# A four-layer graph network on one core: the first feed-forward layer reads unstrided, and the order of work is drawn up anew

## The chip, the core and the metric

The kernel runs on one core of a Trainium2 chip. TensorE (PE) multiplies matrices, VectorE (DVE) and ScalarE (ACT) do elementwise work, GpSimd (POOL) does small sums and issues software DMAs, SyncE (SP) issues most DMAs. SBUF holds tiles of 128 partitions; PSUM has eight banks, into which TensorE writes. The metric is the device time of one execution in microseconds; less is better. Before the change the median of three runs is 2790.44 us (2789.14 to 2792.24).

## What is computed

64 graphs of 256 nodes with 256 features go through four layers; each is followed by a residual and a normalization. The reference, cut to the part that the change touches and the names of the rest:

```python
# layer 0: transformer block, 8 heads, masked by adj, adj transposed or the diagonal
attn_out = ctx @ Wo.T + bo
x = _layernorm(x + attn_out, ln1_g, ln1_b)
ff = jax.nn.relu(x @ W1.T + b1) @ W2.T + b2      # W1: 1024 x 256, W2: 256 x 1024
x = _layernorm(x + ff, ln2_g, ln2_b)
...
x = _layernorm(x + _L0_gnn_ref(x, adj, ...))     # attention and feed-forward
x = _layernorm(x + _L1_gnn_ref(x, adj, ...))     # graph attention, leaky ReLU, softmax
x = _layernorm(x + _L2_gnn_ref(x, adj, ...))     # graph attention, then ELU
x = _layernorm(x + _L3_gnn_ref(x, ..., adj, adj))  # two relation convolutions with ELU
```

All products are fp32. One fp32 matmul appears in the profile as two records; the gathers of layer 3 use a format in which one record is one matmul.

## The kernel before

One graph is some 190 operations: loads, transposes, products, activations. The program does not run them graph after graph. `graph(g)` only notes each operation in a list, with its engine, an assumed cost, the tiles it reads and writes, and for a DMA an assumed delay. Then `Plan.schedule` plays the list through with these assumed costs and gives each engine its order; the instructions are issued in that order and each engine runs its own queue strictly in it. Among the operations that are ready an engine takes the one with the smallest due date. A due date is `DUE[kind] + LATER[graph]`, two tables of numbers written into the file; for TensorE a switch of the array's mode is added, weighted by `WORTH`. Tiles live in rings (`RINGS`) of fixed depth, and the eight PSUM banks are one ring, so an operation may also wait until a buffer is free. Several graphs are in work at once. `LOADED`, `SENT`, `BACK`, `SENT_ROW` and `BACK_ROW` are the assumed delays of DMAs.

TensorE works in modes: `full` for ordinary products (`product`, line 786), `row` for the scores of attention, in which four heads use 32 rows of the array each (line 882), `col` for the values block (lines 903 and 908), `one` for the gathers of layer 3 (line 1066), `bits` for the four transposes that turn the mask (line 824).

Before a product the activations have to lie transposed. For the graphs 0 to 58 this goes through DRAM (`bounced`): DVE transposes 32 x 32 blocks into `turned`, one DMA writes `rows`, a second reads them back as `T`. In `T` the 256 nodes of a graph stand interleaved: column 2m+i is node m of half i. The last `QUICK` = 5 graphs use transposes on TensorE instead, in natural order. `bounced` returns the tile and a function that gives a product its slice:

```python
return xT, lambda kb, i: xT()[:, kb].rearrange("p (m i) -> p i m", i=NB) if i is None else xT()[:, kb, i::NB]
```

With `i` given, the slice is the stationary operand (128 columns, every second one). With `i` None it is the moving operand of the first feed-forward layer, all 256 columns, first the even and then the odd ones, so that the hidden activations `hid` come out in natural order. ACT applies ReLU and writes `hid` (line 943). The second layer takes 128 columns of `hid` at a time as its stationary operand, through `product_plus`, which also serves the product with `Wo`:

```python
y = product_plus(lambda c: hid()[:, c, :], [hid, c_w2], lambda c: w2[:, c, :], NF, x1)
```

Setup loads weights: `wqkv` by twelve DMAs on ACT's queue, and what has to match the block order (`spread`) by four DMAs each on SP's queue.

Of the kernel before, what the change touches and what calls it, by code (L numbers as in the profile page):

```python
# [18 lines left out]
P = 128  # L19
# [6 lines left out]
QUICK = 5  # L26

LOADED = 3.2
SENT, BACK = 1.4, 2.2
SENT_ROW, BACK_ROW = 1.7, 3.2  # L30
# [8 lines left out]
WORTH, HOLD, WAIT = 158.14, 0.22, 23878.4  # L39
DUE = [  # L40
    -228.56, -76, -83.88, -152.17, -246.95, 144.67, -73.58, -50.13, -117.26, -62.43, -95.69, -135.64, -139, -295.21, -282.91, -186.21, -208.41, -104.04, -41.69, 132.39,
    -61.27, -165.13, -39.15, -180, -151.62, -359.77, -136.97, -344.63, -320.09, -212.19, -142.72, -99.05, 49.68, -80.11, -92.33, -82.22, -228.49, -162.34, -196.2, -244.91,
    -216.45, -69.88, -156.28, -117.75, -82.85, -52.68, -193.67, -239.33, -167.89, -289.39, -43.68, -114.12, -6.04, -10.42, -77.71, -92.13, -53.68, -111.24, -22.19, 168.32,
    144.59, 51.01, 8.81, 41.24, 84.37, 175.47, -24.19, 84.36, -61.57, 131.34, 85.1, -80.71, -149.2, -75.32, 8.06, 27.39, 8.04, -267.57, -62.37, -17.58,
    -253.26, 102.77, 33.92, 18.35, -42.69, -46.09, -48.28, -230.96, -240.74, -321.05, -358.53, -500.29, -514.2, -396.36, -557.51, -771.93, -457.43, -478.74, -295.12, -293.77,
    -405.7, -476.74, -352.2, -274.57, -467.78, -231.13, -189.12, -188.57, -269.51, 216.71, -414.44, 85, 252.52, -54.65, 70.81, -26.5, -215.89, 59.94, 28.39, -485.41,
    -154.54, 102.66, 140.08, -147.96, -262.57, -356.35, -119.53, -148.1, -119.88, -155.26, -161.9, 91.8, -6.93, 12.94, 85.56, 162.78, 25.66, 214.61, 205.89, -197.51,
    -182.79, -197.06, -200.26, -103.63, -115.59, -259.31, -338.52, -106.34, -259.71, -80.69, -497.88, 3.42, -248.76, -327.25, -97.33, 8.68, -180.16, -368.65, -281.95, -105.3,
    -275.74, -247.06, 65.77, -233.44, -85.19, -421.05, -566.16, -486.26, -486.32, -451.69, -442.06, -437.05, -494.12, -508.08, -524.83, -535.88, -518.97, -502.94, -406.01, -476.79,
    -603.45, -343.11, -627.7, -347.53, -174.47, -215.44, -307.54, -408, -112.1, 303.26, 157.74, -39.8, 33.34, 19.96, -300.13, -276.05, -318.71, -327.57, -173.95, -392.12,  # L50
    -156.12, 76.61, -274.79, -361.2, -404.53, -442.47, -519.09, -319.99, -321.18, -291.94, -277.27, -97.06, -315.75, -207.94, -305.04, -125.76, -110.74, -169.12, 68.43, -298.22,
    116.97, 182.76, 26.52, -52.2, -168.42, -233.58, 74.87, 51.38, 57.3, -105.14, -38.09, -30.98, 220.31, 2.89, -163.07, -66.56, -178.1, -275.21, -285.22, -154.13,
    -215.98, -40.34, -24.02, -336.24, 87.43, 124.72, 139.7, -183.1, 20.61, 134.12, -103.74, -217.56, 72.34, 27.18, -125.06, -29.64, -87.06, 56.18, -184.37, -327.66,
    -254.51, -77.41, -216.61, 145.97, -178.56, 65.18, 121.01, 65.95, -164.16, 71.23, 298.67, 101.42, 119.26, 246.24, -19.2, 157.71, -60.74, -49.1, 141.16, 151.7,
    6.29, -203.23, -214.07, 282.47, 36.1, 97.36, 73.41, -159.5, 105.08, 245.27, 55.33, -78.57, -96.45, -99.32, -111.3, -40.22, -71.72, 20.46, -93.44, -51.8,
    -82.46, -123.38, -63.03, -174.7, -109.33, -99.49, 7.74, 7.8, -100.27, -107.37, 43.65, 17.73, -91.19, -69.85, 137.33, -70.25, -342.89, -70.97, -208.14, -97.55,
    81.62, -137.39, -254.76, -114.68, -104.47, 10.23, -50.26, -110.2, -73.87, -176.91, -55.18, -138.53, -312.94, 43.31, -61.82, -0.72, -61.78, -74.02, -38.63, -29.27,
    -70.14, -28.91, 41.42, -98.59, -63.24, -125.41, -81.33, -172.67, -267.92, -56.4, -90.76, -104.21, -60.25, -75.66, -341.93, -194.02, -95.39, -42.07, -515.83, -135.12,
    -112.03, -64.06, -106.33, 66.32, 27.41, 24.19, 10.28, -179.06, -86.33, -145.89, -86.5, -68.17, -53.55, -89.7, -37.91, -81.15, -35.28, -26.15, -21.73, -82.24,
    -22.52, 98.51, 16.99, -111.93, 0.44, -329.15, -38.71, -35.42, -23.68, 13.05, -99.5, 44.6, -30.29, 23.99, -167.93, -74.84, 17.01, -27.46, 18.86, -60.34,  # L60
    -114.38, -19.34, -16.53, -27.1, -139.34, -170.9, -168.16, -179.31, -94.74, 188.45, -118.11, -19.49, -66.48, -278.07, -211.79, -4.89, 27.98, -71.67, -104.5, 53.68,
    -44.94, -47.55, -0.25, -35.15, -37.03, 35.19, -57.46, 56.74, -104.02, 95.93, -31.72, -130.63, 56.29, -25.11, -41.73, -33.88, 32.01, 54.42, -106.5, 2.29,
    22.41, -85.35, -124.85, 266.99, -151.39, 28.71, -4.56, -69.98, -154.76, -14.62, -93.54, -203.26, -68.22, -64.68, -222.87, -184.46, 22.24, 35.38, -99.64, -117.5,
    9.44, -97.68, -133.82, -144.02, -66.91, -74.28, -268.84, -284.99, -315.31, -82.83, -92.11, -374.61, -350.77, -338.3, -353.53, -241.11, -152.28, -288.49, -134.99, -213.19,
    -254.85, -13.82, 44.42, -100.57, 96.07, 74.78, 30.02, -55.36, 4.56, -111.81, 16.41, -82.19, -24.85, -85.15, -253.62, -68.59, -23.2, -78.67, -106.02, -70.78,
    -139.17, -118.08, -139.23, -106.7, -220.82, 221.79, -174.78, -173.9, -72.04, -68.83, -153.77, 23.12, 35.07, -159.76, -108.02, -215.02, -42.35, -8.63, 122.93, -75.54,
    -137.89, -45.2, 169, -249.18, -107.96, -108.64, -147.3, -191.12, -193.79, -404.95, -144.89, -230.67, -150.37, -341.69, -237.62, -171.13, -128.84, -32.83, -142.37, -174.5,
    24.25, -2.12, -133.1, -67.37, -46.83, 209.67, -75.45, -161.34, 26.56, 15.42, -226.2, -123.98, -84.4, 53.98, -71.36, -93.39, -52.63, 74.55, 20.98, -37.9,
    -33.61, 304.99, 128.28, -35.36, -8.15, -64.1, 70.08, -36.03, -179.68, 65.32, -162.07, 96.39, -98.5, 99.91, -41.91, -8.13, 93.48, 223.91, -125.72, 10.85,
    -6.25, 127.98, -24.34, -126.77, -38.56, -164.97, -105.72, -226.65, 92.67, -210.8, -211.04, -335.06, -144.72, -469.23, -582.94, -517.45, -247.22, -199.88, -352.97, -129.8,  # L70
    -215.39, -302.48, -253.94, -240.91, -172.2, -35.13, -454.21, -275.89, -41.12, 56.56, 0.62, -109.22, -246.09, 42.23, -124.72, 148.9, -51.41, -108.52, -53.6, 133.5,
    -64.45, -325.5, -94.04, -208.16, -52.22, -100.71, 62.82, -48.49, -82.22, -153.66, 106.74, -139.96, -236.91, 39.55, -74.32, -220.41, -111.57, -250.98, -118.14, -140.76,
    -27.16, 105.12, -174.95, 197.59, 133.52, -56.45, 101.7, 52.32, -86.67, -87.41, 90.45, 44.99, 214.52, 52.63, 95.67, 35.23, -0.08, 151.96, 240.56, 64.62,
    -66.41, 70.67, 2.68, 64.12, -67.27, -6.81, 71.85, -75.35, 200.91, 156.95, -17.7, -141.62, 34.42, -6.02, -194.13, 70.67, 127.66, -117.54, -96.88, -108.28,
    -9.58, -218.12, -6.58, -71.34, -95.78, 16.09, -65.95, -549.11, -29.95, 39.22, 72.42, -117.95, -205.75, -307.48, -94.32, -165.63, 103.33, 66.01, -68.27, -73.44,
    -43.77, -158.66, -227.92, -59.71, -138.35, -139.55, -251.65, -490.14, -183.81, -111.55, -85.37, 130.24, -64.12, -46.91, -38.3, 127.07, -58.84, 230.43, 157.99, 301.55,
    63.64, -280.98, 9.33, -222.5, -149.85, -74.3, -65.46, -104.18, -139.2, -72.03, 1.32, 133.39, 37.1, 145.41, 81.35, -29.58, -85.73, 10.69, -89.57, -155.68,
    29.93, -158.69, -136.5, -266.31, -251.57, -293.75, -343.53, -190.33, -56.18, -67.01, -183.21, -434.13, -665.78, -309.53, -266.4, -392.43, -414.51, -479.73, -314.38, -260.66,
    -245.16, -214.44, -183.13, -308.57, -166.82, -268.27, -81.36, -116.17, -113.56, -410.09, -22.4, -28.51, -237.86, -155.5, -168.47, -61.24, -166.35, 7.17, 219.14, -83.62,
    -50.64, -44.88, -138.06, 137.5, 300.41, 144.25, 219.56, -24.29, 17.09, 28.44, 157.58, 16.65, -96.34, 84.39, 88.66, 212.4, -210.93, 44.08, 150.63, -143.62,  # L80
    47.03, -142.86, 3.57, 187.87, -24.54, -25.24, -206.26, -188.72, -46.69, -169.46, -42.43, -0.74, -106.68, 6.23, 98.16, -27.97, -232.56, -82.77, -72.44, -234.93,
# [33 lines left out]
class Plan:  # L115
# [13 lines left out]
    LOOK = 40  # L129
# [68 lines left out]
    def schedule(self):  # L198
        n = self.kinds()
# [1181 lines left out]
```

## Time and profile before

| | |
|---|---|
| median of three runs | 2790.44 us |
| the profiled execution | 2788.03 us, its span 2786.3 us |
| granted TensorE clock | 0.996 |
| first layer, matmul records (`T,w`) | 2048, mean 390 ns |
| second layer, matmul records (`w,hid`) | 2048, mean 379 ns |
| weight loads of layers 1 and 2 (`gw,T`) | 1024, mean 195 ns |
| scores (`bank<-qk`) | 2048 records, 139.4 us busy |
| DMA | mean 119 GB/s |

The profile is one execution. A group's row names the line, engine, operation, output and inputs, then busy time and the mean duration of one. Matmuls overlap: a record's duration is longer than the distance to the next one, so the pace is read from the starts in the timeline. The span in 40 slices shows TensorE at nine tenths or more in all but the first and the last slice.

### The profile page before, as it was taken

The numbers are of one execution on the slowest core, as the hardware profiler recorded it, in microseconds if no ns is written. First come the engines' busy times: TensorE is split into PE (matmuls) and PEld (weight loads), VectorE is DVE, ScalarE is ACT, GpSimd is POOL, SyncE is SP. The second block draws the span as 40 slices with busy tenths as digits, with TensorE's granted clock in tenths as the row PEclk, the third lists the DMA queues.
The fourth block names the chain that finished last, engine by engine and source line by source line (L and its number), as shares of the span: only waits on it lengthen the run. The fifth ranks groups of instructions, "written<-read, shape, count | busy, mean of one in ns | idle before, by whom it ended". The sixth has DMA issues, their size and how long they took to land.

```text
span 2786.3 us, 48831 instructions
## 1 busy us (share of the span) xinstructions
PE 2749.3 (99%) x15790; PEld 2092.4 (75%) x15790; DVE 2498.9 (90%) x6527; ACT 1588.5 (57%) x3827; POOL 819.9 (29%) x1753
## 2 busy tenths in 40 slices
PE   7999999999999999999999999999999999999997
PEld 5877777777777777777777777777777777777774
DVE  6898899999999998999999999989999999999777
ACT  4455555655655555556556555555565565566567
POOL 3223232332332322323323323223233232232232
PEclk9999999999999999999999999999999999999999
DMA  7454554545545545545445455455454454553121
GB/s 191 110 124 122 129 125 114 139 108 125 136 113 132 129 115 134 124 114 139 114 120 139 116 126 133 113 134 122 114 139 115 119 135 104 132 122 85 43 55 43
DMA packets 612637, 330.45 MB, mean 119 GB/s; under 512 B 394488, under 2 KB 603896, under 8 KB 612376
## 3 DMA queue, kind: packets, MB, share of 16 engines
q1 hardware_dynamic: 566856, 275.46, 36.1%
q0 software_dynamic: 44560, 51.01, 12.2%
q8 instruction: 128, 2.10, 0.3%
q14 instruction: 133, 1.09, 0.1%
q10 hardware_dynamic: 960, 0.79, 0.1%
HBM read 183.12 MB, written 94.23 MB: 100 GB/s over the span
## 4 chain that ended last, share of the span: by engine, by line
PE 90%; DVE 4%; DMA 3%; ACT 2%; issue 1%; POOL 0%; ACTq 0%; SPq 0%; POOLq 0%; DVEq 0%
PE bank L786 75%; PE bank L882 4%; PE bank L908 4%; PE bank L1066 4%; PE bank L903 2%; DMA rows<-turned 1%; DMA T<-rows 1%; PE bank L824 1%; DVE p L890 0%; DMA row<-cols 0%; DMA pf<-row 0%; DVE turned L755 0%; DVE e L992 0%; DVE e L995 0%; ACT X L807 0%
## 5 line engine op out<-in xcount | busy, mean ns | idle before, releaser
L786 PE MATMUL bank<-T,w 128*128 128x256 f32 x2048 | 500.7, 390 | 0.0
L800 POOL TENSOR_SCALAR rstd<-mv 128x2 f32<-128x2 f32 x384 | 98.1, 256 | 1284.8 <-DVE mv L797 1144.8
L786 PE MATMUL bank<-cw,T 128*128 128x512 f32 x1024 | 462.7, 593 | 1.0 <-DMA T<-rows 0.4
L786 PE MATMUL bank<-w,hid 128*128 128x256 f32 x2048 | 461.6, 379 | 1.3 <-ACT hid L943 1.3
L807 ACT ACTIVATE X<-X,rstd 128x256 f32<-128x256 f32 x640 | 348.9, 597 | 196.4 <-POOL rstd L803 187.1
L786 PEld LDWEIGHTS bank<-T,w 128*128 128x128 f32 x2048 | 379.5, 188 | 91.7 <-issue 13.9
L786 PEld LDWEIGHTS bank<-w,hid 128*128 128x128 f32 x2048 | 388.3, 190 | 58.1 <-issue 2.7
L890 DVE TENSOR_TENSOR p<-p,am 128x512 f32<-128x512 f32 x512 | 332.1, 681 | 11.0 <-ACT p L888 9.0
L786 PEld LDWEIGHTS bank<-cw,T 128*128 128x128 f32 x1024 | 198.2, 195 | 188.0 <-issue 177.0
L888 ACT ACTIVATE p<-bank 128x512 f32<-128x512 f32 x512 | 300.3, 607 | 35.3 <-PE bank L882 35.3
L801 POOL TENSOR_TENSOR rstd<-rstd,neghalf 128x2 f32<-128x2 f32 x384 | 294.8, 768 | 32.2
L786 PE MATMUL bank<-h,e 128*128 128x259 f32 x1024 | 260.1, 383 | 3.7 <-ACT e L997 3.6
L786 PE MATMUL bank<-xT,wqkv 128*128 128x256 f32 x1024 | 260.5, 390 | 3.0 <-DMA cw<-in_w_root_dram 3.0
L1053 ACT CAST hi<-bank 128x256 fp32r<-128x256 f32 x256 | 95.1, 372 | 275.8 <-PE bank L786 275.8
L786 PE MATMUL bank<-gw,T 128*128 128x258 f32 x1024 | 246.3, 381 | 0.7 <-ACT T L736 0.7
L943 ACT ACTIVATE hid<-bank,col_b 128x256 f32<-128x256 f32 x512 | 216.5, 473 | 45.8 <-PE bank L786 42.3
L795 DVE BATCH_NORM_STATS2 st<-X 128x6 f32<-128x256 f32 x640 | 236.7, 411 | 3.0
L786 PEld LDWEIGHTS bank<-h,e 128*128 128x128 f32 x1024 | 189.3, 190 | 56.6 <-issue 24.9
L786 PEld LDWEIGHTS bank<-xT,wqkv 128*128 128x128 f32 x1024 | 188.7, 191 | 57.3 <-issue 28.4
L914 DVE RECIPROCAL inv<-bank 128x256 f32<-128x256 f32 x128 | 218.6, 1727 | 8.0 <-PE bank L908 7.9
L786 PEld LDWEIGHTS bank<-gw,T 128*128 128x128 f32 x1024 | 196.5, 195 | 27.8 <-issue 3.8
L1080 ACT ACTIVATE e<-o 128x512 f32<-128x512 f32 x128 | 80.6, 630 | 217.8 <-DVE o L1076 215.9
(129 smaller groups left out, 4758.3 us busy)
## 6 DMA issues: line engine op xcount, KB each, us to landing
rows<-turned SPq DMA_DIRECT2D x295, 256.0 KB
T<-rows SPq DMA_DIRECT2D x295, 256.0 KB
adj<-in_adj_dram SPq DMA_DIRECT2D x128, 256.0 KB
blocks<-in_x_dram SPq DMA_DIRECT2D x256, 64.0 KB
x<-in_x_dram SPq DMA_DIRECT2D x64, 256.0 KB
xr<-in_x_dram SPq DMA_DIRECT2D x64, 256.0 KB
xr<-row_ln_b POOLq DMA_DIRECT2D x64, 256.0 KB, 4.4
x<-row_bo POOLq DMA_DIRECT2D x64, 256.0 KB, 4.8
```

The costliest lines, as they stand in the source:

```text
L786: nc.tensor.matmul(dst, lhsT=lhs(c), rhs=rhs(c), start=(c == 0), stop=(c == n - 1))
L795: nc.vector.bn_stats(stat()[:, i, :], y()[:, i, :])
L800: nc.gpsimd.tensor_scalar(rstd()[:, 0, :], mv()[:, :, 1], 1.0, EPS, op0=ALU.mult, op1=ALU.add)
L801: nc.gpsimd.tensor_tensor(rstd()[:, 0, :], rstd()[:, 0, :], neghalf[:, 0:NB], op=ALU.pow)
L807: nc.scalar.activation(y()[:, i, :], y()[:, i, :], AF.Identity, bias=rstd()[:, 1, i : i + 1], scale=rstd()[:, 0, i : i + 1])
L882: nc.tensor.matmul(s[r]()[:, hg, :], lhsT=qk()[f, KB + hg, kt * P : (kt + 1) * P], rhs=qk()[f, hg, :], start=True, stop=True)
L888: act(0.58, lambda pr=pr, k=k, sr=s[r]: nc.scalar.activation(pr(), sr(), AF.Exp, accum_out=seen_sum[:, k : k + 1]), [s[r]], [pr])
L890: dve(0.60, lambda pr=pr, kt=kt: nc.vector.tensor_tensor(pr(), pr(), am()[:, kt, None, :].to_broadcast([P, KB, N]), op=ALU.mult), [pr, am] ...
L908: nc.tensor.matmul(pc[32 * r : 32 * r + 32, 0, :], lhsT=v()[:, kt, HD * h : HD * (h + 1)], rhs=p[kt, r]()[:, hg, :], start=(kt == 0), stop ...
L914: dve(1.67, lambda hg=hg, pc=pc: nc.vector.reciprocal(inv()[:, hg, :], pc()[:, 1, :]), [pc], [(inv, hg)])
L943: act(0.36, lambda f=f, k=k, ph=ph: nc.scalar.activation(hid()[:, f + k, :], ph()[:, k, :], AF.Relu, bias=b1[:, f + k : f + k + 1]), [ph, ...
L1066: nc.tensor.matmul(pa()[:, 0:n], lhsT=rel()[:, i, j * P : (j + 1) * P], rhs=part()[:, i, 0:n], start=(c == 0), stop=(c == len(terms) - 1))
```

## The change

Four parts. No product, activation or vector operation is added or taken away.

1. `bounced` hands out the whole row of `T` as it lies for the first layer, so `hid` keeps the interleaved order. The second layer takes every second column of `hid` as its stationary slice. The last five graphs keep their natural order.
2. `spread` and the loads of `wqkv` are two DMAs over all 128 partitions each, where there were four over 32.
3. The rules of the order: the tables `DUE` and `LATER` and the weights are new, a window limits how far an engine may run ahead of its oldest waiting operation, the two groups of scores of a graph are held together, and the assumed delays of DMAs are longer.
4. A few assumed costs are corrected.

```diff
-LOADED = 3.2
-SENT, BACK = 1.4, 2.2
-SENT_ROW, BACK_ROW = 1.7, 3.2
+LOADED = 3.8
+SENT, BACK = 2.5, 3.0
+SENT_ROW, BACK_ROW = 2.7, 3.7
...
-WORTH, HOLD, WAIT = 158.14, 0.22, 23878.4
+WORTH, HOLD, WAIT, LOCK = 20.0, 0.0, 1000000.0, -0.5
+WINDOW, FIRST, TAIL = 4.0, 6, 58
...
-                for o in ops[: self.LOOK]:
+                while point[e] < len(queue[e]) and queue[e][point[e]].start is not None:
+                    point[e] += 1
+                limit = float("inf")
+                if point[e] < len(queue[e]) and FIRST < queue[e][point[e]].graph < TAIL:
+                    limit = queue[e][point[e]].order[0] + WINDOW
+                if e == "PE" and held:
+                    if now < until:
+                        later.append(until)
+                    else:
+                        held = None
+                for o in ops:
+                    if o.order[0] > limit and o.graph > FIRST:
+                        continue
+                    if e == "PE" and held and o is not held:
+                        continue
...
+                if e == "PE":
+                    if o is held:
+                        held = None
+                    elif o.pair and o.pair.start is None:
+                        held, until = o.pair, now + o.cost + 0.5 + LOCK
...
-                view = (t[name] if rel is None else t[name][rel]).rearrange("(k b c) n -> b c k n", b=4, c=32)
-                for b in range(4):
-                    plan.op("SP", 0.6, lambda b=b: nc.sync.dma_start(to[b::4], view[b]), 0, [], [(w, (name, b))],
-                            size=view.shape[3] / 1024 * 0.9, lag=2.2)
+                view = (t[name] if rel is None else t[name][rel]).rearrange("(k b c) n -> k c b n", b=4, c=32)
+                for k in range(KB):
+                    plan.op("SP", 0.55, lambda k=k: nc.sync.dma_start(to[:, k, :], view[k]), 0, [], [(w, (name, k))],
+                            size=view.shape[3] / 512 * 0.9, lag=2.4)
...
-                return xT, lambda kb, i: xT()[:, kb].rearrange("p (m i) -> p i m", i=NB) if i is None else xT()[:, kb, i::NB]
+                return xT, lambda kb, i: xT()[:, kb, :] if i is None else xT()[:, kb, i::NB]
...
+                groups[0].pair, groups[1].pair = groups[1], groups[0]
...
-                    pe("full", 0.4275 * n + 0.01, lambda i=i: product(po()[:, i, :], lambda c: lhs(c)[:, i * P : (i + 1) * P], rhs, n),
+                    pe("full", 0.4275 * n + 0.01, lambda i=i: product(po()[:, i, :], lambda c: lhs(c, i), rhs, n),
...
-                y = product_plus(lambda c: hid()[:, c, :], [hid, c_w2], lambda c: w2[:, c, :], NF, x1)
+                hid_at = (lambda c, i: hid()[:, c, i::NB]) if g < B - QUICK else (lambda c, i: hid()[:, c, i * P : (i + 1) * P])
+                y = product_plus(hid_at, [hid, c_w2], lambda c: w2[:, c, :], NF, x1)
```

The tables `DUE` (one number for each kind of operation) and `LATER` (64 numbers, one for each graph) are replaced whole and not printed.

## The prediction

> **What bounds the kernel.** I read the page from the top: busy shares, the chain that ended last, the costliest groups, then TensorE's own waits, and last the timeline of TensorE in a window in the middle.
>
> ```profile
> PE 2749.3 (99%) x15790; PEld 2092.4 (75%) x15790; DVE 2498.9 (90%) x6527; ACT 1588.5 (57%) x3827; POOL 819.9 (29%) x1753
> PE 90%; DVE 4%; DMA 3%; ACT 2%; issue 1%; POOL 0%; ACTq 0%; SPq 0%; POOLq 0%; DVEq 0%
> ```
>
> TensorE (PE) holds 90% of the chain that ended last. Its busy share alone would not say so, since matmul ends are modelled; its waits do:
>
> ```profile
> PE bank L679 <- DMA blocks<-in_x_dram: 6.4, 1, 6.4
> PE bank L824 <- DVE ident_b L427: 5.6, 1, 5.6
> PE bank L786 <- ACT e L997: 3.6, 11, 0.7
> PE bank L786 <- DMA cw<-in_w_root_dram: 3.0, 1, 3.0
> ```
>
> The whole list adds up to 24.8 us of 2786.3, and of these four lines all but the third lie in the first 30 us. Between its waits TensorE is never free, so the time is the sum of what its instructions take, and a change is worth what it takes out of that sum or out of those waits. The granted clock is 0.996.
>
> ```profile
> L786 PE MATMUL bank<-T,w 128*128 128x256 f32 x2048 | 500.7, 390 | 0.0
> L786 PE MATMUL bank<-w,hid 128*128 128x256 f32 x2048 | 461.6, 379 | 1.3 <-ACT hid L943 1.3
> ```
>
> These are the two feed-forward layers: equal shapes and counts (each fp32 matmul is two records), but the first (T,w) is 11 ns longer per record. Records overlap, so I take the pace from the timeline, where a row is start, length, and run:
>
> ```profile
> 1192.53 3.62 PE L786 MATMUL bank<-w,hid 128*128 128x256 f32 x16
> ...
> 1209.20 4.69 PE L786 MATMUL bank<-T,w 128*128 128x256 f32 x20
> ...
> 1217.41 1.13 PE L786 MATMUL bank<-xT,wqkv 128*128 128x256 f32 x4
> 1218.38 0.39 PE L824 MATMUL bank<-ident_b,bits 128*128 128x128 bf16 x4
> 1218.60 1.08 PE L786 MATMUL bank<-wqkv,xT 128*128 128x256 f32 x4
> 1219.52 3.60 PE L786 MATMUL bank<-cw,T 128*128 128x512 f32 x8
> ...
> 1226.50 1.91 PE L786 MATMUL bank<-gw,T 128*128 128x258 f32 x8
> 1228.34 2.01 PE L882 MATMUL bank<-qk 32*128 32x256 f32 x32
> ...
> 1232.20 1.90 PE L786 MATMUL bank<-gw,T 128*128 128x258 f32 x8
> 1233.94 1.89 PE L786 MATMUL bank<-xT,wqkv 128*128 128x256 f32 x8
> ...
> 1262.55 1.07 PE L786 MATMUL bank<-T,w 128*128 128x256 f32 x4
> 1263.46 3.59 PE L786 MATMUL bank<-cw,T 128*128 128x512 f32 x8
> ...
> 1271.40 1.15 PE L882 MATMUL bank<-qk 32*128 32x256 f32 x16
> 1272.47 1.18 PE L786 MATMUL bank<-T,w 128*128 128x256 f32 x4
> 1273.49 1.91 PE L786 MATMUL bank<-gw,T 128*128 128x258 f32 x8
> ```
>
> A run's last record runs out alone, so w,hid has a pace of (3.62-0.379)/15 = 0.216 us and T,w (4.69-0.390)/19 = 0.226.
>
> **1. The first layer without its step.** The first layer read its moving operand with a step of two fp32; w,hid read without one. The gap is 10.3 ns by the timeline and 11 by the page; I take 10.8. Graphs 0 to 58 took the stepped path (the last five use transposes on TensorE): 59 x 32 = 1888 records x 10.8 ns = **20.4 us**, all on the chain.
>
> A rule speaks against this term. The Trainium skill (SBUF — State Buffer, the note on cachelines under "Door 1: The DMA port swizzle") says that SBUF reads at full rate as long as a 16-byte line is hit at least twice, so that a step of up to 4 fp32 is free. A step of two fp32 hits each line twice: by the rule the first layer was at full rate, this term is 0 and my final number 20 us higher. The two layers differ in nothing else that the rows show, so the row decides.
>
> **2. The step in the second layer's stationary slices.** The row nearest is gw,T, whose stationary slices were already stepped by two: 258 columns in (1233.94-1232.20)/8 = 0.2175 us a record, just 258/256 of 0.216. The page gives its weight loads 195 ns, against 190 for w,hid, and they lie beside a 216 ns matmul. Cost 0; bounds 0 and, if the step costs here what it cost the moving side, 20.4 us. ReLU still writes whole rows of hid, and the output comes out in natural order as before.
>
> **3. The new order: changes between array modes.** No compute instruction is added or removed on any engine; I counted the built programs. What changes is who stands beside whom. A single group of scores (x16) takes 1272.47-1271.40 = 1.07 us; two together (x32) run from 1228.34 to 1230.28, 1.94, that is 0.20 less than two single ones. The matmul before a visit is 0.10 longer (gw,T x8: 1.84 before the x32, 1.74 at 1232.20), the one behind it 0.11 (T,w x4: 1.02 at 1272.47, 0.91 at 1262.55). An avoided visit saves 0.41. The order has 101 visits before and 77 after: 24 x 0.41 = **9.8 us**.
>
> The mask's four transposes stand right behind the values block 45 times in the new order and once in the old. At 1217.41 the projection behind a values block takes 0.97, 0.11 over its 0.86. At the one old place (78.73 us) the transposes behind the block take 0.24 instead of 0.22 and the product after them carries no extra 0.11. So 44 x 0.09 = **4.0 us**.
>
> Layer 3's gathers are split into 230 runs instead of 160. Paired, two take 0.95 us (with the 0.19 by which the matmul ahead is cut short), single ones 0.47 each: nothing to 0.02 us a split, **+0.7 us**. Sum of 1 to 3: 20.4+9.8+4.0-0.7 = **33.5 us**.
>
> **4. Queues and waits.** SP issues 14 fewer DMAs and ACT 6 fewer: weight loads that were four quarters of the partitions are now two halves of the row blocks. The start: until TensorE's first matmul 5.6 us, then waits of 3.0, 0.6 and 6.4, and 2.4 us in the first sixteen products (5.98 us where 3.6 would do): 18.0. The 6.4 is the last block load of the second graph, 20th on SP's queue and issued at 24.8 us. In the new order it is 17th with no first- or second-layer weights ahead, by about 15 us (4 block loads at 1.1, then nine at 0.6, then 4 at 1.1), so it lands beside the first graph's attention. On the other side TensorE now opens with a projection, for which x has to be transposed: 8.6 us, somewhat ahead of the 9.2 of now because no mask load stands between the block loads. 8.6+2.4+3 for new waits = 14, 4 less than now; bounds 11 and 22.
>
> The other waits are 9.2 us. I compared how much TensorE work stands between each product and the next that needs it, middle graphs only. It grows nearly everywhere: second layer to layer 1's product 23 to 29 us, aggregate to layer 2's product 17 to 33, layer 2 to the relation layer 17 to 41, last hidden slice to second layer 1.7 to 5. It shrinks on one chain, Wo's product to the first layer, 24.7 to 16.0 at least. That chain needs add 0.7, statistics 1.2, GpSimd's four 1.5, two ACTIVATEs 1.2, a transpose 0.7, and two DMAs of 3.3 (rows to T issue, 1255.31 to 1258.60; the way back taken as equal): 11.9. It holds. What is tighter: the second group of scores takes the PSUM bank that the second layer's last add has just cleared, with 1.08 us of TensorE work between, and the add needs 0.7 on DVE. In the old order banks came back to scores as close (0.96 us), with hardly a wait. I take 12 for 9.2; bounds 4 and 25.
>
> **Sum.** 2786.3-33.5-4.0+2.8 = 2751.6 span. The profiled execution took 2788.03, 1.7 over its span: 2753.3. The median of the runs, 2790.44, is 2.4 above it: 2755.7, rounded to **2755 us**, 1.3% faster.
>
> **Rivals.**
> - *Only the step pays* (18%): the counted visits are avoided but each avoided visit's time comes back as a wait, because the new order packs DVE more tightly. For it: DVE is at 369 of 400 us in the busiest stretch (2100 to 2500). Against it: the distances above. 2790.4-20.4 = 2770.
> - *The step's price moves along* (7%): second-layer records go to 0.226. 2755+20.4 = 2775. Against it: gw,T.
> - *Waits all but vanish* (12%): start 11, others 4: 11 us less, 2744.
> - *Slower: DVE's in-order queue holds the bank* (4%). Place: the add between the second layer and the scores. If one reciprocal (1727 ns in its row) stands ahead of the add in every graph, TensorE waits 59 x 1.73 = 102 us and the time is 2857. From 0.7 us a graph (41/59) it outweighs the whole gain. Against it: what waits DVE causes TensorE now add up to about 1 us after the start.
> - *No change* (2%): the rule on cachelines holds and the visits' saving is eaten: 2788 to 2790.
>
> The forecast itself has 57%. The range has to hold the first and third rivals and the bounds of the waits: **2741 to 2775**. A change under 0.2% (about 5.6 us) is what these runs cannot tell from none. Faster 94%, same 2%, slower 4%.
>
> **What would show it.** T,w at 379 ns a record and 0.216 pace; w,hid unchanged at 379; 77 visits with 51 of x32; TensorE's list of waits near 25 us with no 6.4 us entry. Wrong if w,hid rises to 390, if waits on DVE's add stand before the scores in every graph, or if the period of a graph in the middle (42.4 to 42.6 us now) is not near 41.9.

## The result: the sum moved as forecast, the start got worse, and the waits in the middle went to nothing

The kernel after takes 2743.47 us (median of 4 runs, 2742.12 to 2744.33), the kernel before 2789.79 on the same chip (2786.16 to 2792.24, 4 runs): ratio 0.9835, 95% interval 0.9818 to 0.9852. The forecast was 2755. The profiled execution took 2743.84 us, its span 2742.1, granted clock 0.997.

Busy shares and the chain that ended last, from the page of the kernel after:

```profile
PE 2707.5 (99%) x15790; PEld 2115.3 (77%) x15790; DVE 2464.9 (90%) x6527; ACT 1597.3 (58%) x3827; POOL 943.8 (34%) x1753
PE 96%; DVE 1%; DMA 1%; ACT 1%; issue 0%; ACTq 0%; SPq 0%; POOL 0%; POOLq 0%; DVEq 0%
```

TensorE's share of the chain went from 90% to 96%; the other engines have nearly left it. Next the groups of the two feed-forward layers (busy us, mean ns of one, idle before):

```profile
L812 PE MATMUL bank<-T,w 128*128 128x256 f32 x2048 | 466.0, 380 | 0.0
L812 PE MATMUL bank<-w,hid 128*128 128x256 f32 x2048 | 456.9, 381 | 0.0
L812 PEld LDWEIGHTS bank<-w,hid 128*128 128x128 f32 x2048 | 397.6, 196 | 41.3 <-issue 2.7
```

The first layer fell from 390 to 380 ns a record, and the second, which now reads the stepped slices, did not rise to it. Its weight loads did, from 190 to 196 ns, beside matmuls that leave 216. Then TensorE's waits (us in total, times, longest):

```profile
PE bank L812 <- DVE xT L804: 15.9, 3, 14.7
PE bank L812 <- DMA wqkv<-in_WqkvT_dram: 1.6, 2, 1.4
PE bank L759 <- ACT turned L770: 1.6, 4, 0.8
PE bank L812 <- DVE ctxT L942: 1.2, 1, 1.2
```

The 14.7 is the start: the first matmul waits until x is transposed. The waits in the middle (`ACT e`, `T<-rows`) are gone; between 100 and 2600 us the list is empty. A stretch of the timeline there (start, length, run):

```profile
1232.08 7.13 PE L812 MATMUL bank<-w,hid 128*128 128x256 f32 x32
1239.14 2.01 PE L908 MATMUL bank<-qk 32*128 32x256 f32 x32
1241.08 2.00 PE L812 MATMUL bank<-wo,ctxT 128*128 128x256 f32 x8
```

This is the place that the slower rival feared: the second layer, then both groups of scores. Together they take all eight banks. The second group begins at about 1240.1, and one of its banks is the one that DVE's add clears just before:

```profile
1239.25 0.69 DVE L953 TENSOR_TENSOR X<-bank,X 128x512 f32<-128x512 f32 x1 [1.43 <-PE bank L812]
```

The add ends less than 0.2 us earlier, and nothing waits. From one second layer to the next a graph takes 41.736 us on average over 30 middle graphs (42.557 before), and twenty single graphs lie between 41.72 and 41.75 (42.14 to 43.28 before).

To see where 44.2 us of span went I gave every TensorE operation of both programs the prices of the prediction (pace by shape, 10.8 ns for a stepped record, the extra of a change of mode), added them up, and called what the real starts show beyond that "lost":

| | before | after | difference | forecast |
|---|---|---|---|---|
| priced work (steps 1 to 3) | 2734.8 | 2699.6 | -35.2 | -33.5 |
| lost up to 100 us, first matmul's start included | 20.6 | 23.9 | +3.3 | -4.0 |
| lost from 100 to 2600 us | 9.3 | -0.2 | -9.5 | } +2.8 |
| lost after 2600 us | 9.7 | 6.4 | -3.3 | } |
| behind the last matmul | 12.0 | 12.5 | +0.5 | 0 |
| span | 2786.3 | 2742.1 | -44.2 | -34.7 |

In the middle the prices of before add up to the time of after within 0.2 us in 2500. How the few special records of the setup and the end are priced moves some 3 us between the rows, alike in both programs; the differences hardly depend on it.

### The profile page after: what moved, and what is told of

It is laid out like the page before. It is cut to its first block, busy times and chain, and to the rows that moved or that the text cites. A ratio compares the mean times of both kernels' runs of the same rounds, so it can differ in the third digit from the quotient of the medians.

```text
span 2742.1 us, 48596 instructions
## 1 busy us (share of the span) xinstructions
PE 2707.5 (99%) x15790; PEld 2115.3 (77%) x15790; DVE 2464.9 (90%) x6527; ACT 1597.3 (58%) x3827; POOL 943.8 (34%) x1753
## 3 DMA queue, kind: packets, MB, share of 16 engines
q0 software_dynamic: 44560, 51.01, 12.5%
## 4 chain that ended last, share of the span: by engine, by line
PE 96%; DVE 1%; DMA 1%; ACT 1%; issue 0%; ACTq 0%; SPq 0%; POOL 0%; POOLq 0%; DVEq 0%
PE bank L812 80%; PE bank L908 5%; PE bank L1094 4%; PE bank L935 4%; PE bank L930 2%; PE bank L850 1%; DMA wqkv<-in_WqkvT_dram 1%; DMA adj<-in_adj_dram 0%; PE bank L759 0%; ACT turned L770 0%; DVE p L916 0%; ACTq L660 0%; ACT e L1109 0%; ACT e L1108 0%; DMA blocks<-in_x_dram 0%
## 5 line engine op out<-in xcount | busy, mean ns | idle before, releaser
L826 POOL TENSOR_SCALAR rstd<-mv 128x2 f32<-128x2 f32 x384 | 147.5, 384 | 1406.0 <-DVE mv L823 413.4
L812 PE MATMUL bank<-cw,T 128*128 128x512 f32 x1024 | 469.1, 593 | 0.0
L812 PE MATMUL bank<-T,w 128*128 128x256 f32 x2048 | 466.0, 380 | 0.0
L812 PEld LDWEIGHTS bank<-w,hid 128*128 128x128 f32 x2048 | 397.6, 196 | 41.3 <-issue 2.7
L827 POOL TENSOR_TENSOR rstd<-rstd,neghalf 128x2 f32<-128x2 f32 x384 | 315.3, 821 | 32.0
L812 PE MATMUL bank<-gw,T 128*128 128x258 f32 x1024 | 254.9, 382 | 0.0
L812 PE MATMUL bank<-xT,wqkv 128*128 128x256 f32 x1024 | 252.2, 382 | 1.6 <-DMA wqkv<-in_WqkvT_dram 1.6
L812 PEld LDWEIGHTS bank<-gw,T 128*128 128x128 f32 x1024 | 199.4, 196 | 45.6 <-issue 23.9
L812 PEld LDWEIGHTS bank<-h,e 128*128 128x128 f32 x1024 | 186.8, 190 | 46.1 <-issue 14.7
L1094 PE MATMUL bank<-hi,rel 128*128 128x258 f32 (+1 forms) x512 | 183.0, 365 | 0.1
L781 DVE STREAM_TRANSPOSE turned<-X 128x512 f32<-128x512 f32 x236 | 166.4, 705 | 5.9 <-ACT X L833 5.7
```

The lines of the kernel that those rows point to most:

```text
L781: dve(0.63, lambda: nc.vector.transpose(turned().rearrange("p k (b n i) -> p (k b) i n", b=4, i=NB), xt().rearrange("p i (j c) -> p j i c" ...
L812: nc.tensor.matmul(dst, lhsT=lhs(c), rhs=rhs(c), start=(c == 0), stop=(c == n - 1))
L826: nc.gpsimd.tensor_scalar(rstd()[:, 0, :], mv()[:, :, 1], 1.0, EPS, op0=ALU.mult, op1=ALU.add)
L827: nc.gpsimd.tensor_tensor(rstd()[:, 0, :], rstd()[:, 0, :], neghalf[:, 0:NB], op=ALU.pow)
L1094: nc.tensor.matmul(pa()[:, 0:n], lhsT=rel()[:, i, j * P : (j + 1) * P], rhs=part()[:, i, 0:n], start=(c == 0), stop=(c == len(terms) - 1))
```

## The experiments

Each ran beside the kernel before on its own chip; ratios are to that. The first four shared one chip (before 2793.43 us), the next three another (2789.97), the last a third (2795.98). The record puts the kernel after on none of these, and the kernel before differs by up to 6 us between chips. So where a difference to after is only a few us, the traces carry the argument, not the medians.

### 1. Put the step back on the moving side

Order, loads and everything else of after stay.

```diff
-return xT, lambda kb, i: xT()[:, kb, :] if i is None else xT()[:, kb, i::NB]
+return xT, lambda kb, i: xT()[:, kb].rearrange("p (m i) -> p i m", i=NB) if i is None else xT()[:, kb, i::NB]
...
-hid_at = (lambda c, i: hid()[:, c, i::NB]) if g < B - QUICK else (lambda c, i: hid()[:, c, i * P : (i + 1) * P])
+hid_at = lambda c, i: hid()[:, c, i * P : (i + 1) * P]
```

> The changed kernel with only the step put back: the first layer reads every second column again, the second layer takes unstepped slices; order and everything else as changed. My account (the moving step costs 10.8 ns a record, all of it on TensorE's chain): T,w records rise from 380 to about 390 ns, the pace of a run from 0.216 to 0.227, and the time is 2743.5 + 20.4 = 2764 us. Rival A (the cacheline rule: a step of two fp32 is free): 2743 us. Rival B (the new order has slack that hides part of it): between 2744 and 2757.

Measured: 2763.09 us (2762.36 to 2764.63), ratio 0.9891 (0.9876 to 0.9907). The first layer's group:

```profile
L812 PE MATMUL bank<-T,w 128*128 128x256 f32 x2048 | 485.8, 387 | 0.0
```

That is 19.6 us over after, and 18.7 us over experiment 3, which ran on the same chip and differs in this step alone; 1888 x 10.8 ns makes 20.4. The spans of the profiled executions differ by 19.6 us too (2761.7 and 2742.1). In this order the step costs nearly its full price, so its removal pays it. The run also shows what the order and the loads pay without the step's removal: 30.3 us, beside before on the same chip. Which of the new rules of the order does it, the tables, the window or the longer delays, no run separates.

### 2. The step alone, in the old order

The kernel before with the two slices changed as in the change, old tables and old loads.

```diff
-return xT, lambda kb, i: xT()[:, kb].rearrange("p (m i) -> p i m", i=NB) if i is None else xT()[:, kb, i::NB]
+return xT, lambda kb, i: xT()[:, kb, :] if i is None else xT()[:, kb, i::NB]
...
-y = product_plus(lambda c: hid()[:, c, :], [hid, c_w2], lambda c: w2[:, c, :], NF, x1)
+hid_at = (lambda c, i: hid()[:, c, i::NB]) if g < B - QUICK else (lambda c, i: hid()[:, c, i * P : (i + 1) * P])
+y = product_plus(hid_at, [hid, c_w2], lambda c: w2[:, c, :], NF, x1)
```

> The kernel before with only the step moved from the first layer's moving operand to the second layer's stationary slices; its order and loads are the old ones. My account: 2790 - 20.4 = 2769 us, and TensorE's waits stay as they were (a 6.4 us wait at the start, about ten 0.4 us ones before the gathers). Rival A (step free): 2790. Rival B (a shorter first layer turns old covers into waits): 2773 to 2785, with new waits in TensorE's list.

Measured: 2779.22 us (2776.14 to 2780.17), ratio 0.9950 (0.9935 to 0.9965): 14.2 us gained, not 20.4. The group shows the step's whole price gone:

```profile
L786 PE MATMUL bank<-T,w 128*128 128x256 f32 x2048 | 480.9, 382 | 0.0
```

and its list of waits shows where a part of it went:

```profile
PE bank L786 <- ACT e L998: 5.8, 18, 0.9
...
PE bank L1067 <- DVE lo L1055: 2.5, 5, 1.0
```

`ACT e` was 3.6 us in 11 waits, `DVE lo` 1.1 in one. By the same pricing this run has 20.6 us less work and loses 18.2 us in the middle instead of 9.3. I read it so: the first layer's records had been part of the cover under which the softmax weights `e` of layer 1 are made ready; with 0.35 us less of them in each graph, TensorE gets there earlier than they do. That covers about half of it: of the 8.9 us more, some 4 stand ahead of products that read `e`, some 2.4 ahead of layer 3's gathers and 1.6 ahead of a second layer (estimates from the distances between starts). By the medians about a third of the step's price comes back as waits in the old order (6.2 of 20.4 us). In the new order, by experiment 1, nearly all of it is kept.

### 3. No step anywhere

After, but the second layer's slices are unstepped too; the nodes of a graph then come out of this layer in another order than the reference's, so the output is permuted.

```diff
-hid_at = (lambda c, i: hid()[:, c, i::NB]) if g < B - QUICK else (lambda c, i: hid()[:, c, i * P : (i + 1) * P])
+hid_at = lambda c, i: hid()[:, c, i * P : (i + 1) * P]
```

> The changed kernel with no step anywhere in the feed-forward block: the second layer too takes unstepped slices of hid, so that the nodes of a graph leave it in interleaved order and the output is permuted. It isolates the price of the step in the stationary slices. My account (hidden beside the 216 ns matmul): within 1 us of the changed kernel, 2743 us, weight loads of w,hid back from 196 to 190 ns. Rival (the step costs on this side what it cost on the other): 2743.5 - 20 = 2723 us.

Measured: 2744.44 us (2742.58 to 2745.17), ratio 0.9825 (0.9810 to 0.9840). The second layer's weight loads:

```profile
L812 PEld LDWEIGHTS bank<-w,hid 128*128 128x128 f32 x2048 | 384.9, 190 | 53.3 <-issue 2.7
```

The step in a stationary slice costs 6 ns of a weight load (196 against 190), all of it beside the matmul, and no time.

### 4. The start: wqkv in quarters again

After, with the six loads of `wqkv` over 128 partitions made twelve over 32; same bytes, same order of all work on TensorE.

```diff
-plan.op("ACT", 0.6, lambda k=k, cut=cut, view=view: nc.scalar.dma_start(wqkv[:, k, cut], view[k]),
-        0, [], [(c_wqkv, (part, k))], size=0.5, lag=2.4)
+def quarters(k=k, cut=cut):
+    for a in (2 * k, 2 * k + 1):
+        nc.scalar.dma_start(wqkv[32 * a : 32 * a + 32, :, cut],
+                            t["WqkvT"][a * KB * 32 : (a + 1) * KB * 32, cut].rearrange("(k c) n -> c k n", c=32))
+
+plan.op("ACT", 0.6, quarters, 0, [], [(c_wqkv, (part, k))], size=0.5, lag=2.4)
```

> The changed kernel with the projection weights loaded as before, in twelve loads of 32 partitions instead of six of 128; TensorE's order is unchanged. In the changed kernel the first matmul waits until 14.7 us for x. Theory L (the shape of these loads slows every transfer beside them): x is transposed near 8 us, the first matmul starts at 8 to 9, and the time falls by 4 to 6 us to about 2738. Rival O (the order of the issues on SP and GpSimd's small loads, not the shape, delays x): first matmul still at 14 to 15 us, time 2743.

Measured: 2737.67 us (2737.04 to 2739.35, 5 runs), ratio 0.9801 (0.9788 to 0.9814), 5.8 us below after, and 6.8 below experiment 3 on the same chip. TensorE's timeline at the start, after first:

```profile
14.66 2.08 PE L812 MATMUL bank<-wqkv,xT 128*128 128x256 f32 x4 [14.66 <-DVE xT L804]
16.97 3.32 PE L812 MATMUL bank<-xT,wqkv 128*128 128x256 f32 x8 [0.24 <-DMA wqkv<-in_WqkvT_dram]
```

and with quarters:

```profile
8.36 2.05 PE L816 MATMUL bank<-wqkv,xT 128*128 128x256 f32 x4 [8.36 <-DMA gw<-in_L_WT_dram]
14.42 5.69 PE L816 MATMUL bank<-xT,wqkv 128*128 128x256 f32 x16 [4.02 <-DMA wqkv<-in_WqkvT_dram]
```

The first four loads on SP's queue are the blocks of x in both. In after they take 5.70 us to issue:

```profile
0.74 5.70 SPq L801 DMA_DIRECT2D blocks<-in_x_dram  x4
```

With quarters they take 2.72:

```profile
0.74 2.72 SPq L805 DMA_DIRECT2D blocks<-in_x_dram  x4
```

The waits of SP's queue in the first 16 us say what that time is, in after

```profile
SPq L801 <- DMA wqkv<-in_WqkvT_dram: 4.0, 1, 4.0
```

and with quarters:

```profile
SPq L805 <- DMA blocks<-in_x_dram: 1.0, 1, 1.0
```

A load signals its landing on a semaphore (a counter), and the program reuses a few semaphores in turn. In after the third load of x has the semaphore of the first `wqkv` load, whose last update comes at 5.62 us; the load of x is issued at 5.64. A quarter that was issued at the same time, 0.74 us, lands by 2.85, and there the third load of x has no wait. The last load of x then takes 7.8 us from issue to its last update in after (6.00 to 13.80) and 4.4 with quarters (3.15 to 7.52).

So the loads of `wqkv` on ACT's queue, in their new shape, held up the loads of x on SP's, first by the semaphore and then in the transfer itself: x was transposed at 13.9 us instead of 7.5. Why the new shape lands so late is not tested. In the trace such a load updates its semaphore five times, once early and four times late, and a quarter sixteen times; that would fit a load that four of the 16 DMA engines carry, and then neither the number of partitions nor the size of a transfer would be the cause, but how the load is divided.

TensorE starts 6.3 us earlier, and 4.0 of that goes to a wait for the weights loaded last. About 2.2 us come back between 52 and 57 us, where after still runs at half clock (experiment 7). What is set there is kept: from 77 us to the end every matmul of the two layers lies 5.84 to 5.85 us earlier than in after.

### 5 and 6. The price of a visit

A matmul of one column in the full mode stands between the two groups of scores (5, `kt == 0` is the group that is issued second), or ahead of both (6, the same with `kt == 1`). The same 64 matmuls are added in both; only the first splits the pairs. The line that holds the two groups of a graph together turned out to do nothing: left out of the program, the order on every engine is the same, so the pairs come from the tables.

```diff
+if kt == 0:
+    nc.tensor.matmul(s[0]()[:, 0, 0:1], lhsT=wqkv[:, 0, 0:P], rhs=ident[:, 0:1], start=True, stop=True)
```

> As the kernel after, with one matmul of one column in the full mode put in front of every graph's second-issued group of scores, so that a pair of groups becomes two visits of the row mode. It adds 64 matmuls to the work, which the output does not need. Theory (a visit has a price of 0.41 us that two groups side by side pay once): the 51 pairs become 102 single visits, 21 us, on top of the small matmuls themselves (64 at about 0.22 us, 14 us): about 2743.5 + 35 = 2778. Rival (the switch is hidden and the pairing is worth nothing): only the small matmuls, about 2758, the same as the run with the matmul ahead of the first group.

> The control of the run before: the same 64 added matmuls, but in front of the group of scores that is issued first, where the array is in the full mode anyway, so no visit is split. Theory and rival both: 2743.5 + 64 x 0.22 = 2758. The difference between the two runs is the price of 51 visits: 21 us by the price of 0.41, 0 if the visits are hidden.

Measured: 2770.86 us (2769.87 to 2773.01, 5 runs), ratio 0.9932 (0.9919 to 0.9946), with the pairs split; 2751.55 (2750.42 to 2752.06, 4 runs), 0.9861 (0.9846 to 0.9876), with them whole. The timeline with the pairs split:

```profile
1245.07 7.13 PE L812 MATMUL bank<-w,hid 128*128 128x256 f32 x32
1252.14 1.15 PE L910 MATMUL bank<-qk 32*128 32x256 f32 x16
1253.21 0.38 PE L906 MATMUL bank<-ident,wqkv 128*128 128x1 f32 x2
1253.53 1.15 PE L910 MATMUL bank<-qk 32*128 32x256 f32 x16
```

and with the pair whole:

```profile
1235.87 7.13 PE L812 MATMUL bank<-w,hid 128*128 128x256 f32 x32
1242.84 0.28 PE L906 MATMUL bank<-ident,wqkv 128*128 128x1 f32 x2
1243.05 2.01 PE L910 MATMUL bank<-qk 32*128 32x256 f32 x32
```

From the second layer to the product with `Wo` (1254.60 and 1244.98) it takes 9.53 and 9.11 us: 0.42 for the extra visit. Over the run, by the medians on one chip, the difference is 19.3 us, 0.38 for each of the 51 pairs; 0.41 was forecast, 21 expected. The rival (visits are hidden) is out. The added matmuls came to 8 us, not 14: I had put 0.22 us on each, and it is 0.13 on average.

### 7. The value weights first

The start with quarters, and the part that TensorE waited for at 14.4 us loaded first.

```diff
-for part in range(3):
+for part in (2, 0, 1):
```

> The kernel after with the query, key and value weights in quarters of 32 partitions, as in the run that loaded them so, and the value weights loaded first instead of last. That run had one wait left at its start, 4.0 us at 14.4 us for the weights that were loaded last, which TensorE wants for its second product. Theory (that wait is the order on the queue): it falls to 2 us or less, 2734.5 to 2736. Rival (the bytes of the start arrive no sooner, whatever the order): 2737.7 again, the wait only standing at another product.

Measured: 2738.16 us (2735.12 to 2739.71, 5 runs), ratio 0.9812 (0.9799 to 0.9825): no gain, as the rival said, but not for its reason. The wait did fall, from 4.0 to 0.5 and 0.35, and the first scores start at 18.31 us instead of 21.49. Yet at 77 us this run is 2.1 us behind the run with quarters. The windows of this run show why (TensorE's busy us and records, granted clock, DMA share, GB/s):

```profile
24.00:28.00 4.00, 2.97 (x11) 0.57 1.03 342
28.00:32.00 4.00, 4.00 (x12) 0.57 1.05 358
40.00:44.00 4.00, 2.81 (x16) 0.71 0.98 190
44.00:48.00 4.00, 4.00 (x23) 0.50 0.39 111
48.00:52.00 4.00, 4.00 (x12) 0.51 0.56 154
```

and the run with quarters:

```profile
40.00:44.00 4.00, 2.84 (x16) 0.79 1.07 216
44.00:48.00 4.00, 4.00 (x19) 0.50 0.32 96
48.00:52.00 4.00, 4.00 (x18) 0.85 0.60 177
```

TensorE's clock was halved twice here and once there. A matmul record of 256 columns then follows its predecessor after 0.427 us instead of 0.216. Four times the sum of what the clocks miss of 1.00 is 8.6 us here and 3.4 there. That is an upper bound, since a halved clock costs nothing while TensorE waits; without the waits it is 7.7 and 3.4. Matmul against matmul, this run is 3.2 us ahead at the first scores and 1.9 ahead at 26 us (a wait of 0.98 us for `wo` has come in between); the first halving makes that 0.8 behind, the second 2.1 behind.

The windows print 1.00 for the first microseconds too, but there the trace holds no clock record yet, and the matmuls run at half pace: in the rows of experiment 4 the first four records take 2.08 and 2.05 us, most of them 0.43 apart. Full pace begins at 13.8 us in before, 19.7 in after, 18.5 with quarters and 14.3 here.

The kernel after loses 4.7 to its later halving (5.1 with waits counted in):

```profile
44.00:48.00 4.00, 2.84 (x18) 0.88 1.16 222
48.00:52.00 4.00, 3.26 (x13) 0.50 0.38 104
52.00:56.00 4.00, 4.00 (x10) 0.50 0.61 192
56.00:60.00 4.00, 4.00 (x20) 0.84 0.52 132
```

and the kernel before 5.8 (6.8), from 24 to 38 us.

### 8. Keep the clock up

In the run with quarters the clock falls among 32 setup records with one column each (the shift of the first layer's bias). Here they have 64 equal columns, of which one is used.

```diff
-pf = plan.tile("bank", [P, NF], F32)
+pf = plan.tile("bank", [P, NF, 64], F32)
...
-nc.tensor.matmul(pf()[:, f : f + 1], lhsT=w1[:, c, f * P : (f + 1) * P], rhs=bcol[:, c : c + 1],
+nc.tensor.matmul(pf()[:, f, :], lhsT=w1[:, c, f * P : (f + 1) * P], rhs=bcol[:, c : c + 1].to_broadcast([P, 64]),
...
```

> As the kernel after with the query, key and value weights in quarters, and with the 32 setup matmul records of one column (the shift of the first feed-forward bias) widened to 64 equal columns, of which one is used; same number of instructions, same order. In the run without this the granted TensorE clock stands at 0.50 from about 42.3 to 49 us, right behind these one-column matmuls and one wait of 1.2 us; the windows from 40 to 52 us add up to 3.4 us lost. Theory (the clock falls because matmuls of one column count as hardly any work): the clock stays at 1.00 between 40 and 52 us, or the dip is shorter, and the time is 2734 to 2735.5. Rival (the waits alone bring the clock down): 0.50 again in the same place and 2737.7.

Measured: 2736.55 us (2735.34 to 2740.31, 5 runs), ratio 0.9788 (0.9774 to 0.9801). The same windows:

```profile
40.00:44.00 4.00, 2.94 (x23) 1.00 1.03 199
44.00:48.00 4.00, 2.81 (x20) 1.00 0.41 117
48.00:52.00 4.00, 4.00 (x20) 1.00 0.63 179
```

The clock stays at 1.00, though TensorE waits twice for over 1 us here: the theory holds, the waits alone do not bring it down. All nine other profiled executions have their clock halved between 24 and 48 us; this one has it full from 19.4 us to the end of the matmuls. Where a halving falls also moves with the time at which the narrow records come, so one execution does not settle how many columns are enough. The gain is smaller than the 3.4 us of clock, since a wait of 1.19 us for the second graph's x takes its place; the profiled run is 1.4 us ahead of the run with quarters. By their intervals the two versions can't be told apart. Both beat the kernel after.

## Why the forecast was right in sign and 11.5 us too long

**1, the first layer without its step: right.** 20.4 forecast; experiment 1 measured 19.6 (18.7 on one chip). The row decided against the Trainium skill's rule on cachelines (SBUF — State Buffer, under "Door 1: The DMA port swizzle"), by which this was 0: the records went from 390 to 380 ns. "Only the step pays" (2770) is the wrong way round: the step alone pays 14 us in the old order, and more than it comes with the new one.

**2, stationary slices: right.** Cost 0, by experiment 3. So the rival in which the price moves along is out.

**3, visits and transposes: right.** 33.5 forecast for steps 1 to 3, 35.2 found; the visit's 0.41 measured as 0.38 to 0.42. The transposes' 4.0 and the gathers' 0.7 have no run of their own; only the sum is confirmed.

**4, the start: wrong.** "8.6 us, somewhat ahead of the 9.2 of now because no mask load stands between the block loads" looked at SP's queue alone. The loads of `wqkv` on ACT's queue changed shape in the same change, and I counted that as 6 issues saved. They delayed x by 6 us: the first matmul came at 14.7. With quarters it came at 8.4, close to the 8.6. The step also left out the halved clock, 5.8 us of the old start and 4.7 of the new one. The "2.4 us in the first sixteen products" is the half pace before 13.8 us (records 0.43 apart), read as waits. And "The 6.4 is the last block load of the second graph" is a misreading. The timeline of before has

```profile
26.02 6.95 PE L679 MATMUL bank<-spread_ln_b,w 128*128 128x1 f32 x32 [6.35 <-DMA blocks<-in_x_dram]
```

and these matmuls read no block. They need the first layer's weights, whose last quarter has its last semaphore update at 25.57 us; the block load was issued at 24.80 and landed only after 26.02. The wait went, as forecast, but not for the reason given.

**4, the other waits: wrong, and this is the term that made the forecast too long.** "The other waits are 9.2 us", and "I take 12 for 9.2": lost time after 100 us was 19.0, not 9.2, and fell to 6.2. The list of waits had undercounted, because records overlap. The prediction shows second-layer records starting at 1192.53, sixteen of them; at 0.216 us each the next product could start at 1195.99. It starts here (timeline of the kernel before):

```profile
1196.62 1.15 PE L786 MATMUL bank<-h,e 128*128 128x259 f32 x4 [0.47 <-ACT e L997]
```

0.63 us late, and the list says 0.47: the last record still runs for 0.16 us after its successor could have begun. Every wait is listed 0.16 too short, and since the list begins at gaps of 0.15 us, one under about 0.31 not at all. I had read the longer distances between products ("It grows nearly everywhere") as no reason to count on fewer waits; they took away nearly all there were.

The two errors had opposite signs, 7.3 us too little at the start and 15.6 too much behind it, so part of the nearness of 2755 to 2743 is luck. The time landed on the rival "waits all but vanish" (2744), and that too by luck in part: right about the middle, wrong in giving the start 11 us. One sum beside the forecast is off: the slower rival's 41 us is not the forecast's gain, which is 2790.4 - 2755 = 35.4, or 0.6 us a graph.

## What to carry to other kernels

When a bound engine gets faster, its work is also cover for others: price the removal by the instruction, then ask what was being made ready meanwhile, and expect to reschedule before the full price is paid out. Where records overlap, take lost time from the distances between starts, not from the list of idle gaps. Look at every queue that moves at the start, at which semaphore each load waits for there, and at the granted clock in windows of a few microseconds; a start that is late by 6 us stays late by 6 us for all that follows.

## What was unexpected in the hardware

TensorE's clock fell to half without a long pause. In after it stood at 0.50 from 47 us on, with no gap above 1.2 us in the 15 us ahead of it, but among the last 16 of 32 records of one column:

```profile
42.58 1.50 PE L705 MATMUL bank<-spread_ln_b,w 128*128 128x1 f32 x12
45.24 1.10 PE L812 MATMUL bank<-wo,ctxT 128*128 128x256 f32 x4 [1.16 <-DVE ctxT L942]
46.18 2.65 PE L705 MATMUL bank<-spread_ln_b,w 128*128 128x1 f32 x16
```

Widened to 64 columns in experiment 8, the same records kept it at 1.00. The Trainium skill (TensorE: Matmul & The Clock Gate, the part on the clock gate) ties the halving to an idle window of about 3.4 us; in the kernel before that fits, where TensorE has been waiting for over 4 us when the clock falls at 24.04, here it does not. The wider records hardly took longer, 1.55 us for twelve against 1.50 above:

```profile
39.40 1.55 PE L709 MATMUL bank<-spread_ln_b,w 128*128 128x64 f32 x12
```

Loads over 128 partitions on one queue held up small loads on another, with the same bytes to move: four took 5.70 us to issue instead of 2.72, and 4.0 of that was one wait for a semaphore that such a load held until it had landed.
